# A state-space layer: GpSimd's tensor work moved to VectorE, ScalarE and TensorE, and shorter PSUM tenancies

One NeuronCore of a Trainium2 chip. The metric is the device time of one execution in microseconds (us), lowest is best; "the kernel before" and "the new kernel" are the two sides of the change. The kernel keeps its working tiles in SBUF, the large on-chip memory, and TensorE's products go to PSUM, of which it uses 8 banks; the tenancy of a PSUM tile is the time for which it keeps its banks. The granted clock is the share of full speed that the throttle granted TensorE.

## The reference, cut to what matters

The program is a convolution and attention block, then a bidirectional Mamba layer, then a recurrent layer, on 4 images of 128 channels and 64x64 points. Only the Mamba layer is touched: per direction, 4096 tokens, 4 heads of 64, state of 64.

```python
def _mamba3(x, in_proj, conv_w, conv_b, A_log, dt_bias, D, norm_w, out_proj):
    z, xbc, dt = jnp.split(x @ in_proj, [D_INNER, D_INNER + CONV_DIM], axis=-1)
    xp = jnp.pad(xbc, ((0, 0), (K - 1, 0), (0, 0)))
    xbc = silu(sum((xp[:, i:i + l, :] * conv_w[:, i] for i in range(K))) + conv_b)   # 4 taps
    xh, Bm, Cm = jnp.split(xbc, [D_INNER, D_INNER + D_STATE], axis=-1)
    dt = softplus(dt + dt_bias)
    y = _ssd(xh, dt, -exp(A_log), Bm, Cm) + xh * D      # scores with decays, state carried over chunks
    yg = y * silu(z)
    yn = yg * rsqrt(mean(yg * yg, -1) + EPS) * norm_w
    return yn @ out_proj
```

The kernel uses chunks of 128 tokens, both directions in one pass: 32 chunks an image, 128 in all. Below, "the gate" is the product with silu(z), "the root" the inverse square root of the mean square, BT the transposed B, xdt the inputs times dt, xdd the same times the decay to the chunk's end, and "the exponents" the differences of cumulated decays that the exponential is taken of. Projections and taps are made for groups of four chunks.

## The kernel before: the parts that matter

```python
psj = tile_pool(name="m_psj", bufs=2, space=PSUM)   # projections, one bank each
pst = tile_pool(name="m_pst", bufs=1, space=PSUM)   # tr: 1 bank, pS: 1 bank
psy = tile_pool(name="m_psy", bufs=2, space=PSUM)   # py: 2 banks, twice

def convolved(r, g, i, xc):
    pp = bank()                                     # projection of 512 tokens (cut)
    act(raw[:, i, PAD:], pp, AF.Copy)               # after the pad: gpsimd memset or copy of 3 columns
    nc.gpsimd.tensor_scalar(xc[:, i, :], raw[:, i, PAD:], cw[:, i, PAD:KC], cb[:, i], ALU.mult, ALU.add)
    for tap in range(PAD):
        nc.vector.scalar_tensor_tensor(
            xc[:, i, :], raw[:, i, tap : tap + MG], cw[:, i, tap : tap + 1], xc[:, i, :], ALU.mult, ALU.add)

def front(r, c):                                    # chunk c: all that does not need the state
    # 4 DMA of the cumulated decays into cbc; 4 transposes into ptr; xdt = ptr * dt on VectorE
    nc.gpsimd.tensor_tensor(xdd, xdt, tail, ALU.mult)
    nc.tensor.transpose(py[:, 0, DI + P :], xc[:, 0, cols], k.ident); act(BT, py[:, 0, DI + P :], AF.Copy)
    for d in range(ND): nc.tensor.matmul(py[:, d, DI : DI + P], ...)         # scores, then gm = scores * tri
    for d in range(ND):
        for h in range(NHEAD):
            nc.vector.tensor_scalar(lt[:, d, h, :], cbc[:, d, h, :], s1, s1, ALU.min, ALU.subtract)
    act(lt, lt, AF.Exp); nc.vector.tensor_tensor(lt, lt, gm, ALU.mult); act(E, cbc[:, ND], AF.Exp)
    nc.gpsimd.tensor_copy(dec, E[:, :, P - 1 : P]); nc.gpsimd.tensor_tensor(E, E, C, ALU.mult)

def scan(r, c, v, S):                               # 16 products into py, 2 into pS
    nc.gpsimd.tensor_tensor(S1, S, dec, ALU.mult); nc.vector.tensor_tensor(S1, S1, pS, ALU.add)
    # y = xc * D + py (4 on VectorE)
    nc.gpsimd.tensor_tensor(y, y, zs, ALU.mult)     # the gate

def back(b, c, v):
    act(sq, y, AF.Square)
    nc.gpsimd.tensor_tensor(sq[:, :, 0, :], sq[:, :, 0, :], sq[:, :, 1, :], ALU.add)
    # mean square: 2 products into py; rms; root on GpSimd; 4 output products into py; 2 updates of t on VectorE

for c in range(-1, NT + 1):                         # order of issue
    back(b, c - 1, ...); vs[c + 1] = front(r, c + 1); S = scan(r, c, vs[c], S)
    next(pj, None)                                  # a pair of projections with taps, or gate projections
```

## Time and profile before

| | kernel before |
|---|---|
| time, median of 4 runs beside the new kernel | 5501.5 us (5500.4 to 5503.6) |
| the layer, from 3130 us to the last gate less 5 us | 2119 us |
| TensorE in it: busy, idle, granted clock | 1575, 544, 0.69 |
| VectorE, ScalarE, GpSimd busy | 1459, 632, 1099 us |

The layer is cut at the last product with the gate, less 5 us, in every kernel, so that the layers can be compared. Busy is the union of an engine's instructions; idle is the rest of the window. Six of the 128 gate products lie before 3130 us, so the window holds some 122 chunks; where the layer is divided by 128 for a time per chunk, that time is some 5% low.

### The profile page before, as it was taken

The numbers are of one execution on the slowest core, as the hardware profiler recorded it, in microseconds if no ns is written. First come the engines' busy times: TensorE is split into PE (matmuls) and PEld (weight loads), VectorE is DVE, ScalarE is ACT, GpSimd is POOL, SyncE is SP. The second block draws the span as 40 slices with busy tenths as digits, with TensorE's granted clock in tenths as the row PEclk, the third lists the DMA queues.
The fourth block names the chain that finished last, engine by engine and source line by source line (L and its number), as shares of the span: only waits on it lengthen the run. The fifth ranks groups of instructions, "written<-read, shape, count | busy, mean of one in ns | idle before, by whom it ended". The sixth has DMA issues, their size and how long they took to land. (4 is left out here: it accounts for less than half of the span.)

```text
span 5493.2 us, 46592 instructions
## 1 busy us (share of the span) xinstructions
PE 4679.7 (85%) x17552; PEld 2096.2 (38%) x17552; DVE 2544.0 (46%) x4768; ACT 1367.5 (25%) x1959; POOL 1255.0 (23%) x1383
## 2 busy tenths in 40 slices
PE   6999999999999999999997677777777777777777
PEld 2333333333333333333333334443344334434446
DVE  4222232223232323232323866676657676777665
ACT  2112121212121211121211322332233322322245
POOL 0000000000000000000000555455545554555530
PEclk9999999999999999999997776667766776777678
DMA  2000000000000000000000211111112121121101
GB/s 103 0 0 0 0 1 0 0 0 0 0 0 0 0 0 0 0 0 0 0 0 11 54 43 47 43 47 46 47 40 49 46 47 41 49 52 47 49 5 63
DMA packets 70716, 128.35 MB, mean 23 GB/s; under 512 B 16720, under 2 KB 19664, under 8 KB 69200
## 3 DMA queue, kind: packets, MB, share of 16 engines
q1 hardware_dynamic: 65664, 115.63, 8.0%
q10 hardware_dynamic: 4816, 9.65, 0.5%
q8 instruction: 139, 2.28, 0.2%
q14 instruction: 97, 0.79, 0.1%
HBM read 115.80 MB, written 9.44 MB: 23 GB/s over the span
## 5 line engine op out<-in xcount | busy, mean ns | idle before, releaser
L247 PE MATMUL pc<-xp,w 128*128 128x512 f32 x3136 | 1362.7, 595 | 0.0
L247 PEld LDWEIGHTS pc<-xp,w 128*128 128x128 f32 x3136 | 591.3, 189 | 766.1 <-issue 766.1
L234 DVE TENSOR_TENSOR den<-den,ex 128x1024 f32<-128x1024 f32 x448 | 549.0, 1225 | 665.3 <-ACT ex L225 640.9
L223 PE MATMUL pf<-theta,phi 64*128 64x512 f32 x2048 | 805.8, 629 | 0.0
L225 ACT ACTIVATE ex<-pf 128x1024 f32<-128x1024 f32 x512 | 497.6, 1022 | 793.9 <-PE pf L223 793.9
L254 POOL TENSOR_TENSOR t<-t,r 128x512 f32<-128x512 f32 x32 | 40.4, 1264 | 2690.1 <-ACT r L253 2690.1
L227 PE MATMUL acc<-ex,gT 128*64 128x512 f32 x2048 | 550.6, 617 | 67.5 <-ACT ex L225 67.5
L234 DVE TENSOR_TENSOR den<-ex 128x1024 f32<-128x1024 f32 x32 | 39.2, 1225 | 1169.3 <-ACT ex L225 1169.3
L604 DVE SCALAR_TENSOR_TENSOR xc<-raw,cw,xc 128x512 f32<-128x512 f32 x576 | 476.0, 879 | 204.6 <-POOL xc L602 204.6
L223 PEld LDWEIGHTS pf<-theta,phi 64*128 64x128 f32 x2048 | 250.3, 185 | 546.3 <-issue 545.2
L668 DVE TENSOR_SCALAR lt<-cbc,s 128x128 f32<-128x128 f32 x1024 | 435.2, 477 | 7.7 <-PE py L696 7.6
L253 ACT ACTIVATE r<-pc,bsum 128x512 f32<-128x512 f32 x32 | 22.0, 687 | 1465.6 <-PE pc L251 1465.6
L485 ACT ACTIVATE BT<-py 128x128 f32<-128x128 f32 x128 | 35.5, 277 | 1183.9 <-PE py L654 1183.9
L696 PE MATMUL py<-lt,xdt 128*64 128x128 f32 x2048 | 264.0, 396 | 58.7 <-DVE lt L673 58.2
L736 PE MATMUL py<-wout,y 128*128 128x128 f32 x1024 | 236.3, 371 | 68.5 <-DVE t L739 53.9
L227 PEld LDWEIGHTS acc<-ex,gT 128*64 128x64 f32 x2048 | 102.0, 135 | 468.7 <-ACT ex L225 276.2
L594 PE MATMUL pj<-un,full 128*128 128x512 f32 x256 | 221.7, 972 | 53.9 <-ACT raw L485 47.7
L736 PEld LDWEIGHTS py<-wout,y 128*128 128x128 f32 x1024 | 195.4, 261 | 166.6 <-DVE t L739 84.0
L729 PE MATMUL py<-ones,sq 128*128 128x1 f32 x512 | 105.9, 311 | 179.3 <-POOL sq L726 178.0
L696 PEld LDWEIGHTS py<-lt,xdt 128*64 128x64 f32 x2048 | 169.6, 196 | 201.9 <-DVE lt L673 110.1
L717 POOL TENSOR_TENSOR y<-y,zs 128x512 f32<-128x512 f32 x128 | 164.3, 1283 | 305.7 <-DVE y L714 299.0
L602 POOL TENSOR_SCALAR xc<-raw,cw,cb 128x512 f32<-128x512 f32 x192 | 220.7, 1158 | 42.5 <-ACT raw L485 42.4
(190 smaller groups left out, 5076.7 us busy)
## 6 DMA issues: line engine op xcount, KB each, us to landing
cbc<-csd SPq DMA_DIRECT2D x256, 256.0 KB, 4.5
cbc<-csd SPq DMA_DIRECT2D x256, 128.0 KB, 4.5
t<-in_x SPq DMA_DIRECT2D x4, 2048.0 KB, 26.5
out<-t SPq DMA_DIRECT2D x2, 2048.0 KB, 18.3
out<-t ACTq DMA_DIRECT2D x2, 2048.0 KB, 18.5
w<-in_w7t ACTq DMA_DIRECT2D x1, 3136.0 KB, 15.5
w<-in_w5t ACTq DMA_DIRECT2D x1, 1600.0 KB, 23.8
csd<-cs SPq DMA_DIRECT2D x16, 64.0 KB, 1.6
```

The costliest lines, as they stand in the source:

```text
L223: nc.tensor.matmul(pf[:, h, :], phi[half, m, :], theta[half, cols], start=True, stop=True)
L225: nc.scalar.activation(ex, pf, AF.Exp, scale=scale)
L227: nc.tensor.matmul(acc[h * IC : (h + 1) * IC], gT[:, 2 * m + h, :], ex[:, h, :], start=(m == 0), stop=(m == NT // 2 - 1),)
L234: nc.vector.tensor_tensor(den, ex0 if m == 1 else den, ex, ALU.add)
L247: nc.tensor.matmul(pc, w7[:, y, x, :], xp[:, q * RW + y : (q + 1) * RW + y, x : x + W], start=(y + x == 0), stop=False,)
L594: nc.tensor.matmul(pp, full[:, d, DI + h * P : DI + (h + 1) * P], own(r["un"], d, g), start=True, stop=True)
L602: nc.gpsimd.tensor_scalar(xc[:, i, :], raw[:, i, PAD:], cw[:, i, PAD:KC], cb[:, i], ALU.mult, ALU.add)
L604: nc.vector.scalar_tensor_tensor(xc[:, i, :], raw[:, i, tap : tap + MG], cw[:, i, tap : tap + 1], xc[:, i, :], ALU.mult, ALU.add)
L668: nc.vector.tensor_scalar(lt[:, d, h, :], cbc[:, d, h, :], r["s1"][:, d, c, h : h + 1], r["s1"][:, d, c, h : h + 1], ALU.min, ALU.subtract,)
L696: nc.tensor.matmul(o, v["xdt"][:, d, h, :], v["lt"][:, d, h, :], start=True, stop=S is None)
L717: nc.gpsimd.tensor_tensor(y, y, zs[:, :, :, cols], ALU.mult)
L736: nc.tensor.matmul(po, y[:, d, h, :], wout[:, d, h, :], start=(h == 0), stop=(h == 1))
```

## The change

Its intent is to empty GpSimd's queue of all but the gate, the roots and a few small fixes, and to let the next chunk's front begin without the last one's back. The core of the diff:

```diff
-            act(raw[:, i, PAD:], pp, AF.Copy)
-            nc.gpsimd.tensor_scalar(xc[:, i, :], raw[:, i, PAD:], cw[:, i, PAD:KC], cb[:, i], ALU.mult, ALU.add)
+            act(xc[:, i, :], pp, AF.Identity, scale=cw[:, i, PAD:KC], bias=cb[:, i])
             for tap in range(PAD):
+                o = PAD - tap
                 nc.vector.scalar_tensor_tensor(
-                    xc[:, i, :], raw[:, i, tap : tap + MG], cw[:, i, tap : tap + 1], xc[:, i, :], ALU.mult, ALU.add
+                    xc[:, i, o:], pp[:, 0 : MG - o], cw[:, i, tap : tap + 1], xc[:, i, o:], ALU.mult, ALU.add
                 )
+            nc.vector.tensor_copy(ends[g % 2][:, i, :], pp[:, MG - PAD :])
+            # (once a group: six small GpSimd operations add the last group's ends to the first 3 columns)
...
-            py = v["py"] = psy.tile([P, ND, NC], F32, tag="py", name="py")      # held from scores to output
+            pf = pst.tile([P, ND, NC], F32, tag="pf", name="pf")                # transposes and scores; py in scan, po in back
-            nc.gpsimd.tensor_tensor(xdd, xdt, r["tail"]..., ALU.mult)
+            nc.vector.tensor_tensor(xdd, px, r["tail"]..., ALU.mult)            # tail is multiplied by dt beforehand
...
-                    nc.vector.tensor_scalar(lt[:, d, h, :], cbc[:, d, h, :], s1, s1, ALU.min, ALU.subtract)
-            act(lt, lt, AF.Exp)
+                    if d == 0:
+                        nc.vector.tensor_scalar(x, x, s1, 0.0, ALU.add, ALU.max)
+                    else:
+                        act(x, x, AF.Relu, bias=s1)
+            act(cbc, cbc, AF.Exp, scale=-1.0)
-            nc.gpsimd.tensor_tensor(E, E, xc[:, 1, cols]..., ALU.mult)
+            nc.vector.tensor_tensor(CE, E, xc[:, 1, cols]..., ALU.mult)
...
-                nc.gpsimd.tensor_tensor(S1, S, v["dec"]..., ALU.mult)
-                nc.vector.tensor_tensor(S1, S1, pS, ALU.add)
+                for h in range(NHEAD):
+                    nc.vector.scalar_tensor_tensor(S1[:, h, :], S[:, h, :], v["E"][:, h, P - 1 : P], pS[:, h, :], ALU.mult, ALU.add)
...
-            nc.gpsimd.tensor_tensor(sq[:, :, 0, :], sq[:, :, 0, :], sq[:, :, 1, :], ALU.add)
+            # mean square: 4 accumulating products in place of 2 (8 records of the trace a chunk in place of 4)
...
-                if c >= 1: back(...)        # was ahead of front and scan
                 front(...); scan(...)
+                if c >= 1: back(...)        # now behind them
```

Not shown: the decays are stored negated; exponents and decays are worked in place in cbc, which gets three buffers in place of two; and GpSimd's copy of the last decay (dec, 85 us) falls away.

More of the change, by code (lines that the diff above doesn't have):

```diff
@@ L470, in mamba @@
             nc.vector.tensor_tensor(wout, wout, nw.unsqueeze(3).to_broadcast([P, ND, 2, P]), ALU.mult)
-        raw = wp.tile([P, 6, PAD + MG], F32, name="raw")
+        ends = [wp.tile([P, 6, PAD], F32, name=f"ends{i}") for i in range(2)]
         unp = ctx.enter_context(tc.tile_pool(name="m_un", bufs=NG + 2))
@@ L480, in mamba @@
         pst = ctx.enter_context(tc.tile_pool(name="m_pst", bufs=1, space=PSUM))
-        psy = ctx.enter_context(tc.tile_pool(name="m_psy", bufs=2, space=PSUM))
         def act(out, in_, func, **kw):
@@ L562, in prepare @@
             act(tail, pa, AF.Exp)
+            nc.vector.tensor_tensor(tail, tail, dt, ALU.mult)
             pc = bank()[:, 0 : ND * NT * NHEAD].rearrange(dims, d=ND, c=NT)
@@ L572, in prepare @@
                 cs = tmp.tile([P, 2 * P], F32, tag="cs", name="cs", bufs=2)
-                nc.vector.tensor_copy(cs, pr)
+                nc.vector.tensor_scalar(cs, pr, -1.0, None, ALU.mult)
                 for i in range(2):
@@ L596, in convolved @@
                 )
-            if g == 0:
-                nc.gpsimd.memset(raw[:, i, 0:PAD], 0.0)
-            else:
-                nc.gpsimd.tensor_copy(raw[:, i, 0:PAD], raw[:, i, MG : MG + PAD])
-            act(raw[:, i, PAD:], pp, AF.Copy)
-            nc.gpsimd.tensor_scalar(xc[:, i, :], raw[:, i, PAD:], cw[:, i, PAD:KC], cb[:, i], ALU.mult, ALU.add)
+            act(xc[:, i, :], pp, AF.Identity, scale=cw[:, i, PAD:KC], bias=cb[:, i])
             for tap in range(PAD):
+                o = PAD - tap
                 nc.vector.scalar_tensor_tensor(
-                    xc[:, i, :], raw[:, i, tap : tap + MG], cw[:, i, tap : tap + 1], xc[:, i, :], ALU.mult, ALU.add
+                    xc[:, i, o:], pp[:, 0 : MG - o], cw[:, i, tap : tap + 1], xc[:, i, o:], ALU.mult, ALU.add
                 )
+            nc.vector.tensor_copy(ends[g % 2][:, i, :], pp[:, MG - PAD :])
         def project(r, g):
@@ L615, in project @@
                 convolved(r, g, i + 1, xc)
-                yield
+                if i < 4:
+                    yield
+            if g > 0:
+                for tap in range(PAD):
+                    n = PAD - tap
+                    m = grp.tile([P, 6, PAD], F32, tag="m", name="m")
+                    nc.gpsimd.tensor_tensor(
+                        m[:, :, 0:n], ends[(g - 1) % 2][:, :, tap:], cw[:, :, tap : tap + 1].to_broadcast([P, 6, n]), ALU.mult
+                    )
+                    nc.gpsimd.tensor_tensor(xc[:, :, 0:n], xc[:, :, 0:n], m[:, :, 0:n], ALU.add)
+            yield
             for i in range(0, 6, 2):
@@ L634, in front @@
             xc, _ = r[g]
-            v = {}
-            cbc = wk.tile([P, ND + 1, NHEAD, P], F32, tag="cbc", name="cbc")
+            cbc = wk.tile([P, ND + 1, NHEAD, P], F32, tag="cbc", name="cbc", bufs=3)
             for d in range(ND):
@@ L640, in front @@
                 nc.sync.dma_start(cbc[d * DS : (d + 1) * DS, ND], src[1:2].to_broadcast([DS, NHEAD, P]))
-            ptr = pst.tile([P, ND, DI], F32, tag="tr", name="ptr")
+            pf = pst.tile([P, ND, NC], F32, tag="pf", name="pf")
             for i in range(4):
-                nc.tensor.transpose(ptr[:, i // 2, bass.ts(i % 2, P)], xc[:, 2 + i, cols], k.ident)
-            heads = [P, ND, NHEAD, HD]
-            xdt = wk.tile(heads, F32, tag="xdt", name="xdt")
-            nc.vector.tensor_tensor(
-                xdt, ptr.rearrange("p d (h c) -> p d h c", h=NHEAD),
-                r["dt"][:, :, c, :].unsqueeze(3).to_broadcast(heads), ALU.mult,
-            )
@@ L650, in front @@
-            xdd = wk.tile(heads, F32, tag="xdd", name="xdd")
-            nc.gpsimd.tensor_tensor(xdd, xdt, r["tail"][:, :, c, :].unsqueeze(3).to_broadcast(heads), ALU.mult)
-            py = v["py"] = psy.tile([P, ND, NC], F32, tag="py", name="py")
-            nc.tensor.transpose(py[:, 0, DI + P :], xc[:, 0, cols], k.ident)
-            BT = wk.tile([P, P], F32, tag="BT", name="BT")
-            act(BT, py[:, 0, DI + P :], AF.Copy)
+                nc.tensor.transpose(pf[:, i // 2, bass.ts(i % 2, P)], xc[:, 2 + i, cols], k.ident)
@@ L657, in front @@
+            nc.tensor.transpose(pf[:, 0, DI + P :], xc[:, 0, cols], k.ident)
             for d in range(ND):
                 half = slice(d * DS, (d + 1) * DS)
-                nc.tensor.matmul(py[:, d, DI : DI + P], xc[half, 0, cols], xc[half, 1, cols], start=True, stop=True)
+                nc.tensor.matmul(pf[:, d, DI : DI + P], xc[half, 0, cols], xc[half, 1, cols], start=True, stop=True)
+            heads = [P, ND, NHEAD, HD]
+            px = pf[:, :, 0:DI].rearrange("p d (h c) -> p d h c", h=NHEAD)
@@ L660, in front @@
+            xdt = wk.tile(heads, F32, tag="xdt", name="xdt")
+            nc.vector.tensor_tensor(xdt, px, r["dt"][:, :, c, :].unsqueeze(3).to_broadcast(heads), ALU.mult)
+            xdd = wk.tile(heads, F32, tag="xdd", name="xdd")
+            nc.vector.tensor_tensor(xdd, px, r["tail"][:, :, c, :].unsqueeze(3).to_broadcast(heads), ALU.mult)
             gm = wk.tile([P, ND, P], F32, tag="gm", name="gm")
             nc.vector.tensor_tensor(
-                gm, py[:, :, DI : DI + P], k.tri.unsqueeze(1).to_broadcast([P, ND, P]), ALU.mult
+                gm, pf[:, :, DI : DI + P], k.tri.unsqueeze(1).to_broadcast([P, ND, P]), ALU.mult
@@ L663, in front @@
             )
-            lt = wk.tile([P, ND, NHEAD, P], F32, tag="lt", name="lt")
             for d in range(ND):
                 for h in range(NHEAD):
-                    nc.vector.tensor_scalar(
-                        lt[:, d, h, :], cbc[:, d, h, :],
-                        r["s1"][:, d, c, h : h + 1], r["s1"][:, d, c, h : h + 1], ALU.min, ALU.subtract,
-                    )
-            act(lt, lt, AF.Exp)
-            nc.vector.tensor_tensor(lt, lt, gm.unsqueeze(2).to_broadcast([P, ND, NHEAD, P]), ALU.mult)
@@ L674, in front @@
-            E = wk.tile([P, NHEAD, P], F32, tag="E", name="E")
-            act(E, cbc[:, ND], AF.Exp)
-            dec = wk.tile([P, NHEAD, 1], F32, tag="dec", name="dec")
-            nc.gpsimd.tensor_copy(dec, E[:, :, P - 1 : P])
-            nc.gpsimd.tensor_tensor(E, E, xc[:, 1, cols].unsqueeze(1).to_broadcast([P, NHEAD, P]), ALU.mult)
-            v.update(xdt=xdt, xdd=xdd, BT=BT, lt=lt, dec=dec, CE=E)
-            return v
+                    x, s1 = cbc[:, d, h, :], r["s1"][:, d, c, h : h + 1]
@@ new lines, in front @@
+                    if d == 0:
[3 more added lines that the diff above has]
+            act(cbc, cbc, AF.Exp, scale=-1.0)
+            BT = wk.tile([P, P], F32, tag="BT", name="BT")
+            act(BT, pf[:, 0, DI + P :], AF.Copy)
+            lt, E = cbc[:, 0:ND], cbc[:, ND]
+            nc.vector.tensor_tensor(lt, lt, gm.unsqueeze(2).to_broadcast([P, ND, NHEAD, P]), ALU.mult)
@@ L682, in scan @@
+            CE = wk.tile([P, NHEAD, P], F32, tag="CE", name="CE")
+            nc.vector.tensor_tensor(CE, E, xc[:, 1, cols].unsqueeze(1).to_broadcast([P, NHEAD, P]), ALU.mult)
+            return dict(xdt=xdt, xdd=xdd, BT=BT, lt=lt, E=E, CE=CE)
         def scan(r, c, v, S):
@@ L686, in scan @@
             xc, zs = r[g]
-            py = v["py"]
+            py = pst.tile([P, ND, NC], F32, tag="py", name="py")
             pS = pst.tile([P, NHEAD, HD], F32, tag="pS", name="pS")
@@ L707, in scan @@
             else:
-                nc.gpsimd.tensor_tensor(S1, S, v["dec"].to_broadcast([P, NHEAD, HD]), ALU.mult)
-                nc.vector.tensor_tensor(S1, S1, pS, ALU.add)
+                for h in range(NHEAD):
+                    nc.vector.scalar_tensor_tensor(
+                        S1[:, h, :], S[:, h, :], v["E"][:, h, P - 1 : P], pS[:, h, :], ALU.mult, ALU.add
+                    )
             y = wk.tile([P, ND, 2, P], F32, tag="y", name="y")
@@ L721, in back @@
         def back(b, c, v):
-            y, py = v["y"], v["py"]
+            y = v["y"]
+            po = pst.tile([P, NC], F32, tag="po", name="po")
             sq = wk.tile([P, ND, 2, P], F32, tag="sq", name="sq", bufs=1)
             act(sq, y, AF.Square)
-            nc.gpsimd.tensor_tensor(sq[:, :, 0, :], sq[:, :, 0, :], sq[:, :, 1, :], ALU.add)
-            pms = py[:, 0, DI : DI + ND]
+            pms = po[:, ND * P : ND * P + ND]
             for d in range(ND):
-                nc.tensor.matmul(pms[:, d : d + 1], sq[:, d, 0, :], k.ones[:, 0:1], start=True, stop=True)
+                for h in range(2):
+                    nc.tensor.matmul(
+                        pms[:, d : d + 1], sq[:, d, h, :], k.ones[:, 0:1], start=(h == 0), stop=(h == 1)
+                    )
             rms = wk.tile([P, ND], F32, tag="rms", name="rms")
@@ L733, in back @@
             for d in range(ND):
-                po = py[:, d, DI + P : DI + 2 * P]
+                pd = po[:, bass.ts(d, P)]
                 for h in range(2):
-                    nc.tensor.matmul(po, y[:, d, h, :], wout[:, d, h, :], start=(h == 0), stop=(h == 1))
+                    nc.tensor.matmul(pd, y[:, d, h, :], wout[:, d, h, :], start=(h == 0), stop=(h == 1))
                 i = c if d == 0 else NT - 1 - c
                 tt = t[:, ds(b * T + i * P, P)]
-                nc.vector.scalar_tensor_tensor(tt, po, rms[:, d : d + 1], tt, ALU.mult, ALU.add)
+                nc.vector.scalar_tensor_tensor(tt, pd, rms[:, d : d + 1], tt, ALU.mult, ALU.add)
         def run(gen):
@@ L770, in mamba @@
                         pj = project(r1, 0)
-                if c >= 1:
-                    back(b, c - 1, vs.pop(c - 1))
                 if f < NT:
@@ L776, in mamba @@
                     S = scan(r, c, vs[c], S)
+                if c >= 1:
+                    back(b, c - 1, vs.pop(c - 1))
                 next(pj, None)
```

## The prediction

> **What bounds the kernel now.** The busy digits of the page come first, to find the stage that the change touches (40 slices of 137 us each; only `mamba`, the state-space layer, is changed).
>
> ```profile
> PE   6999999999999999999997677777777777777777
> DVE  4222232223232323232323866676657676777665
> POOL 0000000000000000000000555455545554555530
> PEclk9999999999999999999997776667766776777678
> ```
>
> From the 23rd slice VectorE jumps from 2 to 6 or 7 tenths, GpSimd from 0 to 5, and the granted TensorE clock falls. That is the layer: about 3130 to 5260 us, some 2130 us or 39% of the span. It runs 128 chunks (4 images of 32), so 16.6 us each. The window totals, next, have columns window, length, then busy us (and instructions) of PE, PE weight loads, DVE, ACT, POOL, then granted clock, DMA share and GB/s:
>
> ```profile
> 0.00:3130.00 3130.00, 2926.10 (x8552) 1079.54 (x8554) 938.13 (x1023) 613.71 (x709) 120.89 (x144) 0.98 0.02 7
> 3130.00:5260.00 2130.00, 1581.02 (x8042) 892.82 (x8038) 1462.90 (x3170) 633.00 (x993) 1102.06 (x1206) 0.69 0.18 45
> ```
>
> In the layer's row (the second) no engine is full: TensorE 74% at a clock of 0.69, VectorE 69%, GpSimd 52%, ScalarE 30%. Over 128 chunks that is 12.4, 11.4, 8.6 and 4.9 us of work in 16.6. So the stage is bound by engines that wait for one another, in order. Who waits is in the waits of 3200 to 5200 us (2000 us; columns: waiter, who is waited for, us, times, longest):
>
> ```profile
> DVE t L739 <- PE py L736: 182.3, 147, 3.0
> DVE xc L604 <- POOL xc L602: 182.3, 160, 5.7
> DVE rms L731 <- PE py L729: 52.5, 32, 3.8
> DVE gm L661 <- PE py L659: 42.9, 44, 1.8
> ...
> PE py L729 <- POOL sq L726: 151.4, 78, 3.7
> ...
> PE py L654 <- DVE t L739: 41.6, 94, 0.7
> PE py L659 <- ACT BT L485: 38.5, 109, 0.4
> ```
>
> VectorE loses 182 us to the convolution's first tap, which GpSimd makes, and some 280 us to the output chain of the chunk before (square sum on GpSimd, mean square, output product, update of t). TensorE's L654 waits for t because one PSUM tile, py, holds a chunk from its score product to its output product, and has two copies: the front of chunk c+1 can't start before the back of c-1 is done. The chain of work that ended last shows the same ring, in one pass of it:
>
> ```profile
> 4953.91 1.33 POOL E L678
> 4955.24 3.08 POOL xc L602 x2
> 4958.32 0.58 POOL S L708
> 4958.90 1.14 POOL sq L726
> 4960.04 0.04 issue
> 4960.08 1.01 PE py L729 x4
> ```
>
> GpSimd holds six microseconds of it without a break: it is busy half the time but everything queues behind it.
>
> **What the Trainium skill says.** (1) "SBUF — State Buffer", Who interferes with whom: a VectorE instruction with two SBUF inputs, or in its two-port mode, contends with GpSimd's reads. The trace agrees: adding two 128x1024 tensors takes 1225 ns in the first stage (L234), where GpSimd idles, and 1465 ns here (L673); a tap seen alone takes 750 ns and 879 on average. (2) "ScalarE: Activation LUTs", What ACT_TABLE_LOAD costs: each per-partition operand adds about 93 ns. The trace agrees: a 128x128 activation with a bias takes 368 ns (L900), without 277 (BT). (3) "PSUM — Partial Sum Buffer" says GpSimd cannot reach PSUM, and to guard PSUM by bank. This is why the old kernel copies the projection to SBUF first; the banks are counted below. (4) "TensorE: Matmul & The Clock Gate", Part 1: the clock gate follows how busy TensorE has been. Here it is 0.98 in the dense first stage and 0.69 in this one, so a denser TensorE may also get faster.
>
> **The change part by part**, in busy us over the stage, from these rows of the page and the grouped instructions:
>
> ```profile
> L604 DVE SCALAR_TENSOR_TENSOR xc<-raw,cw,xc 128x512 f32<-128x512 f32 x576 | 476.0, 879 | 204.6 <-POOL xc L602 204.6
> L668 DVE TENSOR_SCALAR lt<-cbc,s 128x128 f32<-128x128 f32 x1024 | 435.2, 477 | 7.7 <-PE py L696 7.6
> L729 PE MATMUL py<-ones,sq 128*128 128x1 f32 x512 | 105.9, 311 | 179.3 <-POOL sq L726 178.0
> L602 POOL TENSOR_SCALAR xc<-raw,cw,cb 128x512 f32<-128x512 f32 x192 | 220.7, 1158 | 42.5 <-ACT raw L485 42.4
> ```
>
> GpSimd loses L602 221, E times C 187 (128 x 1.46), xdd 135, square sum 117, decayed state 85, dec 85 and the pad copies 78: 908 us. It gets the fix of the first three columns: 28 groups x 6 small operations x an estimated 0.6 us (the small dec and raw copies take 0.45 to 0.67), 100 us. It ends near 330 of 1130.
>
> VectorE: the taps read PSUM and one SBUF tensor. The same operation from PSUM on 128 columns takes 351 ns (L739); a column costs 1.01 ns (xdt: 680 ns for 512 columns of PSUM, gm: 422 for 256), so 384 more make 351 + 387, about 740. I use 745. So 576 x (879-745) saves 77. Half of the 1024 exponents leave: 218. The other 512 run against a quieter GpSimd, 342 instead of 477 ns (342 is what a like operation of that shape, L833, takes in the last stage): 69, of which I count 50, since neighbours overlap (the group's 435 us are 425 each, not 477). L673 back to 1230 ns saves 30. Added: xdd 128 x 0.68 (as xdt, same form) = 87; CE 128 x 0.69 = 88; the state in four operations of 64 columns, 4 x 0.284 (351 less 64 columns) against one of 0.41 = 93; the saved ends 192 x 0.15 = 29. Sum -375 + 297 = -78: from 1463 busy to about 1385, 10.8 us a chunk. The intent is not less VectorE work, but less waiting.
>
> ScalarE: the projection's Copy gets two per-partition operands, 192 x 0.18 = +35; 512 Relus at 0.37 = +189; one exponential of 1536 columns instead of two (1.05 and 0.62) saves the fixed part of one, an estimated 0.19, so 24. +200, from 4.9 to 6.5 us a chunk: under half busy.
>
> TensorE: the square sum moves into the mean-square product, 512 more records like L729: +106 us, all of it on an engine that is at 75%. Nothing else is added. 12.4 becomes 13.2 us a chunk at the old clock.
>
> PSUM keeps 8 banks: 2 projection, 1 transposes, 1 state, 2 x 2 py become 2 projection, 2 pf, 2 py, 1 state, 1 po. The front no longer waits for the back of two chunks ago, and the back now comes after the scan, with a whole chunk of slack for gate, square and root. The price: a projection bank is held through the first tap (0.77), three taps (2.2) and the saved ends (0.15), 3.2 us where it was 0.6.
>
> The scheduled order of the new kernel shows what runs beside what in a chunk with projection. First half: VectorE does xdt, xdd, gm, four exponents, S, y, lt and CE (0.68 + 0.68 + 0.42 + 1.37 + 1.14 + 1.36 + 1.23 + 0.69 = 7.6 us, near 7 with overlap). TensorE does the projection pair (4 records, 0.5 each where the timeline shows the clock full and 1.0 where not: 2 to 4), five transposes (1), the mean square (8 x 0.15 = 1.2), scores (0.5 to 0.8) and state products (1.1): 5.8 to 8.1. Second half: VectorE does the root's input, six taps, two updates of t and two ends (0.15 + 4.5 + 0.7 + 0.3 = 5.6); TensorE the scan and output products (timeline: 16 x 0.141 + 16 x 0.089 + 8 x 0.153 = 4.9). The halves are close, so each engine waits a little in turn. Every fourth chunk has no taps, but the gate's projections.
>
> **The sum.** VectorE's waits come to some 600 us of 2000 now. The 182 for L602 and 23 for the state go, and of the 305 for the back and front products I take half away; new waits for PSUM give some back. That leaves 300 to 450 us idle beside 1385 busy, a stage of 1690 to 1840, or 13.2 to 14.4 us a chunk. TensorE needs 13.2 at the old clock; as it gets denser I put its clock at 0.75 to 0.8 and its work at 12.3 us, a guess from the two stages' clocks. I choose 13.9 us a chunk: 2.7 x 128 = 345 us saved, 5500 - 345 = 5155.
>
> **The rivals.** *PSUM takes the wait over*: both projection banks are held by taps, and transposes of the next image and the gate's projections share them, so TensorE, strictly in order, stops before them. For it: 3.2 us of tenancy, five times the old. Against: the order gives the taps the whole scan as cover. At 1.5 us in each of 96 projecting chunks it costs 145 us: 5300. *ScalarE joins the chain*: its order is Relus, exponential, transposed B, square, first taps, each behind a different engine, so a late DMA or exponent delays the taps. For: +200 us. Against: it is idle 70% now. 1.5 us a chunk would make 5345. *Balance better than I think*: clock near 0.85 and VectorE at 90%: 12.3 us a chunk, 4950. *TensorE bound*: its +106 at an unmoved clock and 95% use gives 13.9, the same time as mine but a different story. Slower than before needs over 3 us of new waits a chunk.
>
> **Range and chances.** Between the two bad rivals together (5400) and the good one (4950), with most weight on single effects: 5030 to 5320. Faster by over 2% means under 5390: 0.89; within 0.09; slower 0.02.
>
> **What would show it.** Right: GpSimd near 15% of the stage, VectorE over 78%, taps near 745 ns, the remaining exponents near 345, L654-like waits for t gone, clock above 0.72. Wrong: long waits of TensorE for VectorE before the projection (first rival), of VectorE's lt or taps for ScalarE (second), taps in PSUM well above 745 ns, or a clock that stays at 0.69 with TensorE over 90% busy (the fourth).

## The result, and the profile after

The new kernel takes 5139.9 us (median of 4 runs, 5129.3 to 5152.5) beside 5501.5. Ratios here are the mean time of one kernel's fast runs over that of the other's fast runs of the same rounds, so not quite the ratio of the medians quoted. It is 0.9343 (95% interval 0.9322 to 0.9364). The prediction was 5155, range 5030 to 5320.

Busy digits of the page of the new kernel, 128 us a slice:

```profile
PE   6999999999999999999999968888888888888877
...
DVE  4231322323123232322323157767676767677765
...
POOL 0000000000000000000000001111111111111120
PEclk9999999999999999999999967878787878788888
```

GpSimd has gone from 5 tenths to 1; TensorE is up from 7 to 8, and its clock from 6 or 7 to 7 or 8. Window totals of the layer (columns as in the prediction), the kernel before, then the new kernel:

```profile
3130.00:5249.00 2119.00, 1574.68 (x8008) 888.37 (x8005) 1458.79 (x3148) 632.37 (x992) 1098.58 (x1202) 0.69 0.18 46
```

```profile
3130.00:4892.00 1762.00, 1472.24 (x8427) 915.23 (x8427) 1262.45 (x3415) 791.57 (x1350) 286.94 (x405) 0.81 0.22 54
```

The layer is 357 us shorter, the kernel about as much, so nothing else moved. Read on TensorE, the difference splits without a remainder: its idle time falls from 544 to 290 us (-254) and its busy time from 1575 to 1472 (-102), although it has 512 records more. The busy time falls with the higher clock: the durations of all its records in the layer sum to 3476 us before and to 3008 after without the added mean-square records, 13.5% less; in inverse proportion to the clocks, 0.695 and 0.806, it would be 13.8%. The projection products show it most strongly, in the groups of the page of the kernel before and of the new one:

```profile
L594 PE MATMUL pj<-un,full 128*128 128x512 f32 x256 | 221.7, 972 | 53.9 <-ACT raw L485 47.7
```

```profile
L594 PE MATMUL pj<-un,full 128*128 128x512 f32 x256 | 141.6, 661 | 52.9 <-DVE ends L603 42.7
```

972 ns each have become 661, for the same 256 records. Not every group follows: the output products take 371 ns before (L736) and 376 after (L742). Now the groups of the new kernel (window 3130 to 4900, shapes kept apart), for the prediction's terms:

```profile
L733 PE MATMUL po<-ones,sq 128*128 128x1 f32 x976 | 154.3, 279 | 1.6 <-DVE t L745 1.6
L484 ACT ACTIVATE cbc<-cbc,s 128x128 f32<-128x128 f32 x484 | 153.4, 394 | 2.4 <-DMA cbc<-csd 2.4
...
L678 DVE TENSOR_TENSOR cbc<-cbc,gm 128x1024 f32<-128x1024 f32 x121 | 150.0, 1240 | 36.9 <-ACT cbc L484 36.9
...
L671 DVE TENSOR_SCALAR cbc<-cbc,s 128x128 f32<-128x128 f32 x484 | 131.2, 330 | 34.0 <-DMA cbc<-csd 34.0
L600 DVE SCALAR_TENSOR_TENSOR xc<-pj,cw,xc 128x511 f32<-128x511 f32 x176 | 129.8, 741 | 0.0
...
L710 DVE SCALAR_TENSOR_TENSOR S<-S,cbc,pS 128x64 f32<-128x64 f32 x476 | 102.7, 274 | 0.0
...
L620 POOL TENSOR_TENSOR m<-ends,cw 128x12 f32<-128x12 f32 x26 | 6.6, 255 | 1.8
```

And the waits of the new kernel, 3200 to 4840 us (1640 us), VectorE's, TensorE's and one of ScalarE's:

```profile
DVE t L745 <- PE po L742: 191.4, 167, 2.7
DVE xdt L659 <- PE pf L655: 67.4, 23, 5.0
...
PE pf L651 <- ACT BT L484: 80.2, 62, 2.9
PE pS L702 <- ACT BT L484: 65.2, 27, 4.4
PE pj L594 <- DVE ends L603: 34.2, 55, 1.6
...
ACT BT L484 <- DVE gm L663: 206.6, 34, 8.1
```

No engine waits for GpSimd's taps, state or square sum any more. VectorE still waits for output products. New is that TensorE waits 145 us for BT, ScalarE's copy of the transposed B. In 65 of them it is the state product (L702), which needs BT. The other 80 are the next chunk's transposes (L651), which need nothing of BT but its place: pf has one copy, and BT is read out of it, after VectorE's gm from the same tile. That is PSUM tenancy again. The chain that ended last shows a second way in which BT comes late, once in a group of four chunks (start, length, what):

```profile
4517.87 1.17 ACT cbc L484 x4
4519.03 9.85 issue
4528.89 1.48 ACT cbc L484
4530.37 0.17 ACT BT L484
4530.54 0.04 issue
4530.59 1.12 PE pS L702 x4
```

After its four Relus ScalarE stands 9.85 us. The view calls it "issue", but the timeline has the answer: VectorE runs its own four exponents of that chunk from 4527.93 to 4528.80, because the scheduler put them behind taps and xdt, and the exponential needs them. BT could have run at 4528.02, when gm was done, but it stands behind that exponential in ScalarE's queue, and TensorE's state product behind BT.

### The profile page after: what moved, and what is told of

It reads as the page before. It is cut to its first block, busy times and chain, and to the rows that moved or that the text cites. A ratio compares the mean times of both kernels' runs of the same rounds, so it can differ in the third digit from the quotient of the medians.

```text
span 5138.3 us, 47952 instructions
## 1 busy us (share of the span) xinstructions
PE 4588.5 (89%) x18064; PEld 2131.6 (41%) x18064; DVE 2342.6 (46%) x5080; ACT 1540.2 (30%) x2343; POOL 390.0 (8%) x531
## 5 line engine op out<-in xcount | busy, mean ns | idle before, releaser
L600 DVE SCALAR_TENSOR_TENSOR xc<-pj,cw,xc 128x510 f32<-128x510 f32 (+2 forms) x576 | 411.6, 739 | 2.8 <-ACT xc L484 2.8
L697 PE MATMUL py<-cbc,xdt 128*64 128x128 f32 x2048 | 325.2, 344 | 15.8 <-DVE y L717 8.0
L484 ACT ACTIVATE cbc<-cbc 128x1536 f32<-128x1536 f32 x128 | 189.9, 1483 | 198.4 <-issue 195.9
L697 PEld LDWEIGHTS py<-cbc,xdt 128*64 128x64 f32 x2048 | 204.4, 168 | 107.1 <-issue 46.9
L742 PE MATMUL po<-wout,y 128*128 128x128 f32 x1024 | 243.1, 376 | 5.2 <-DVE t L745 3.5
L702 PE MATMUL pS<-xdd,BT 128*64 128x256 f32 x512 | 147.7, 504 | 84.8 <-ACT BT L484 75.8
L742 PEld LDWEIGHTS po<-wout,y 128*128 128x128 f32 x1024 | 183.4, 253 | 79.8 <-issue 51.3
L745 DVE SCALAR_TENSOR_TENSOR t<-po,rms,t 128x128 f32<-128x128 f32 x256 | 89.7, 351 | 259.4 <-PE po L742 216.3
L651 PE MATMUL pf<-ident,xc 128*128 128x128 f32 x512 | 106.9, 324 | 101.2 <-ACT BT L484 98.5
L594 PE MATMUL pj<-un,full 128*128 128x512 f32 x256 | 141.6, 661 | 52.9 <-DVE ends L603 42.7
```

Of the source, the lines that this page charges most:

```text
L484: tc.keep_in_program_order(nc.scalar.activation(out, in_, func, **kw))
L594: nc.tensor.matmul(pp, full[:, d, DI + h * P : DI + (h + 1) * P], own(r["un"], d, g), start=True, stop=True)
L600: nc.vector.scalar_tensor_tensor(xc[:, i, o:], pp[:, 0 : MG - o], cw[:, i, tap : tap + 1], xc[:, i, o:], ALU.mult, ALU.add)
L697: nc.tensor.matmul(o, v["xdt"][:, d, h, :], v["lt"][:, d, h, :], start=True, stop=S is None)
L702: nc.tensor.matmul(pS[d * DS : (d + 1) * DS], v["BT"][:, d * DS : (d + 1) * DS], v["xdd"][:, d], start=True, stop=True)
L742: nc.tensor.matmul(pd, y[:, d, h, :], wout[:, d, h, :], start=(h == 0), stop=(h == 1))
```

## The experiments

Eleven of the kernels below are the new kernel with an edit, one is the kernel before with an edit; all gave correct results and were timed in three rounds against the kernel before. "Against new" is the difference of the ratios times 5500 us; the new kernel's own ratio is 0.9343. Each ratio is uncertain by 9 to 12 us either way, and where batches differ, ratios of different chips are compared, so a difference under some 15 us is not shown; the 17 us of u_taps are at that edge. The layer's columns are the window totals as above, of the one profiled run; it is some 20 us off the median for u_sq (5199, slow side) and d_set (5237, fast side), up to 16 for the others.

| run | ratio (95%) | against new | layer us | TensorE busy / idle, clock | VectorE | GpSimd |
|---|---|---|---|---|---|---|
| before | 1 | +361 | 2119 | 1575 / 544, 0.69 | 1459 | 1099 |
| new | 0.9343 (0.9322 to 0.9364) | 0 | 1762 | 1472 / 290, 0.81 | 1262 | 287 |
| u_taps | 0.9374 (0.9358 to 0.9390) | +17 | 1766 | 1461 / 305, 0.80 | 1313 | 555 |
| u_gates | 0.9296 (0.9279 to 0.9313) | -26 | 1723 | 1457 / 266, 0.81 | 1120 | 731 |
| u_exps | 0.9393 (0.9377 to 0.9409) | +28 | 1781 | 1474 / 307, 0.81 | 1364 | 288 |
| u_psum | 0.9358 (0.9343 to 0.9374) | +8 | 1778 | 1458 / 320, 0.78 | 1278 | 302 |
| u_sq | 0.9404 (0.9389 to 0.9420) | +34 | 1823 | 1481 / 342, 0.78 | 1310 | 440 |
| u_taps_gates | 0.9526 (0.9510 to 0.9542) | +101 | 1860 | 1535 / 325, 0.76 | 1283 | 980 |
| u_pool | 0.9831 (0.9815 to 0.9847) | +268 | 2020 | 1531 / 489, 0.72 | 1260 | 1065 |
| b_psum | 0.9787 (0.9771 to 0.9804) | +244 | 2021 | 1574 / 447, 0.71 | 1399 | 1059 |
| d_set | 0.9561 (0.9545 to 0.9577) | +120 | 1859 | 1508 / 351, 0.78 | 1309 | 1062 |
| d_read | 0.9735 (0.9719 to 0.9751) | +216 | 1993 | 1574 / 419, 0.75 | 1469 | 1023 |
| d_pe | 0.9596 (0.9575 to 0.9616) | +139 | 1883 | 1614 / 269, 0.79 | 1263 | 289 |
| n_gates | 0.9248 (0.9232 to 0.9265) | -52 | 1717 | 1464 / 253, 0.82 | 1140 | 728 |

### One part undone at a time

The theory at this point: waits, on GpSimd's queue and on the PSUM tile, were the cost. The rival, which the windows suggest at first sight: VectorE lost some 200 us of work, and the gain is that.

u_taps:

```diff
-            act(xc[:, i, :], pp, AF.Identity, scale=cw[:, i, PAD:KC], bias=cb[:, i])
+            # pad by GpSimd, then:
+            act(raw[:, i, PAD:], pp, AF.Copy)
+            nc.gpsimd.tensor_scalar(xc[:, i, :], raw[:, i, PAD:], cw[:, i, PAD:KC], cb[:, i], ALU.mult, ALU.add)
             # the three taps on VectorE read raw again; no ends, no fix of the first columns
```

> The new kernel with one part undone: the projection is copied to SBUF by ScalarE, the first tap is made by GpSimd, the other taps read SBUF (as before); everything else stays new. It puts about 300 us back on GpSimd and some 64 us on VectorE (taps at 826 ns busy each instead of 715, if the contention comes back). My theory (the time was in waits on GpSimd and on the PSUM tile, not in VectorE's work): VectorE waits for GpSimd's first tap again, 130 to 180 us; time 5270 to 5320. Rival (the gain is the 198 us of VectorE work that fell away): only the 64 us come back, about 5205.

Measured: 5147 us, +17. Both theories expected more. VectorE waits 17 us for GpSimd's first tap (31 times), where it waited 182 before: GpSimd, with only this and the gate to do, is early.

u_gates:

```diff
-            nc.vector.tensor_tensor(tail, tail, dt, ALU.mult)
-            nc.vector.tensor_tensor(xdd, px, r["tail"]..., ALU.mult)
+            nc.gpsimd.tensor_tensor(xdd, xdt, r["tail"]..., ALU.mult)
-            nc.vector.tensor_tensor(CE, E, ..., ALU.mult)
+            nc.gpsimd.tensor_tensor(CE, E, ..., ALU.mult)
-                    (four scalar_tensor_tensor for S1)
+                nc.gpsimd.tensor_tensor(S1, S, v["E"][:, :, P - 1 : P]..., ALU.mult)
+                nc.vector.tensor_tensor(S1, S1, pS, ALU.add)
```

> The new kernel with xdd, E times C and the decayed state put back on GpSimd (the state is then added on VectorE); everything else stays new. GpSimd gets about 400 us, VectorE loses about 220 (xdd 82, E times C 83, three of four state operations 54). My theory: the scan again waits for GpSimd, and the ring through GpSimd comes back in part: slower, 5200 to 5290. Rival (VectorE work sets the time): faster by 100 to 200, 4950 to 5040.

Measured: 5105 us, 26 faster than new. My theory has the sign wrong. The rival has the sign but not the size: VectorE lost 142 us of work and the time 26. So this part of the change, by itself, does harm.

u_exps:

```diff
-                    if d == 0:
-                        nc.vector.tensor_scalar(x, x, s1, 0.0, ALU.add, ALU.max)
-                    else:
-                        act(x, x, AF.Relu, bias=s1)
+                    nc.vector.tensor_scalar(x, x, s1, 0.0, ALU.add, ALU.max)
```

> The new kernel with all eight exponents of a chunk on VectorE, as before, none on ScalarE. VectorE gets 512 x 0.3 = 150 us, ScalarE loses 153. My theory (VectorE is 71% busy, so part of it falls into idle time; ScalarE's late exponential may even wait longer for VectorE): +60 to +100, 5200 to 5240. Rival (VectorE work sets the time): +150 or more, 5290.

Measured: 5159 us, +28, with 101 us more work on VectorE. Less than either expected. With u_gates it rules the rival out: 101 us more VectorE work cost 28, 142 less gained 26.

u_psum:

```diff
+        psy = tile_pool(name="m_psy", bufs=2, space=PSUM)
+            ptr = pst.tile([P, ND, DI], F32, tag="tr", name="ptr")          # x transposes only
-            pf = pst.tile([P, ND, NC], F32, tag="pf", name="pf")
+            pf = psy.tile([P, ND, NC], F32, tag="py", name="py")            # also used by scan and back
+                if c >= 1: back(...)      # ahead of front again
```

> The new kernel with the old tenancy and order: transposes in a bank of their own, one double-buffered two-bank tile that holds a chunk from score product to output product, and the back of chunk c-1 issued ahead of the front of chunk c+1. No engine's work changes. My theory: TensorE's transposed B and scores wait for t again and VectorE for the output chain; half of the old 305 us: 5260 to 5320, and the granted clock falls below 0.78 in the layer. Rival (work on VectorE): no change, 5140.

Measured: 5143 us, +8, and the intervals overlap: no difference shown. The waits do come back (TensorE's transposed B for t 49 us, VectorE's rms for the mean square 91 us), but they replace others. The expected 120 to 180 us were wrong.

So no single part pays, and my theory in its first form falls. Either none of these matters, or they stand in for one another.

### Parts undone together, and the other side

> The new kernel with everything that left GpSimd put back on it together: copy and first tap, xdd, E times C, decayed state, square sum. New stay the PSUM tiles, their order and the exponents' halves. First four runs: each undone part alone cost nothing (0.930 to 0.939 of the kernel before, against 0.934), so the parts stand in for one another. Theory now: GpSimd's in-order queue binds only when it carries all of it (about 1000 us of the layer); then 5330 to 5480. Rival: the PSUM tenancy together with any lighter part is what counts; then GpSimd's load doesn't matter and the time stays 5140 to 5200.

u_pool is u_taps, u_gates and u_sq (next) in one; the dec copies stay out, so not quite everything is back. Measured: 5406 us, +268: three quarters of the whole gain is lost by three edits that cost 17, -26 and 34 alone. GpSimd carries 1065 us (1099 before). TensorE's waits of u_pool, 3200 to 4800 us:

```profile
PE po L722 <- POOL sq L719: 158.7, 76, 5.3
PE pf L642 <- ACT BT L484: 94.5, 44, 5.5
PE pS L693 <- ACT BT L484: 84.0, 21, 5.7
```

The square sum is there a simple addition, but it stands at the end of a full queue and TensorE stands behind it, 151 us in the kernel before too.

u_sq:

```diff
             act(sq, y, AF.Square)
+            nc.gpsimd.tensor_tensor(sq[:, :, 0, :], sq[:, :, 0, :], sq[:, :, 1, :], ALU.add)
-            (mean square from both halves, 4 products)
+            (mean square from sq[:, d, 0, :], 2 products)
```

> The new kernel with the square sum alone back on GpSimd (117 us there; TensorE loses half of the mean-square records, about 77 us). GpSimd theory: not loaded enough to bind, so 5100 to 5150 and, as TensorE is 84% busy, perhaps a gain of up to 40. Rival (this one step was the critical one, since it stands in the output chain): 5200 to 5280.

Measured: 5175 us, +34: between the two expectations. In the profiled run, which is 24 us above the median, TensorE has 457 records fewer and is still busy 9 us longer, at a clock of 0.78, and it waits 62 us for the sum.

b_psum:

```diff
 (the kernel before)
-        psy = tile_pool(name="m_psy", bufs=2, space=PSUM)
+        (front writes transposes and scores to pf, scan has its own py, back its own po, all single; back is issued last)
```

> The kernel before with the new PSUM tiles and the new order alone (front, scan, back; tiles pf, py, po); no engine's work changes. GpSimd theory: the ring through GpSimd stays, 5400 to 5500. PSUM rival: most of the gain comes, 5150 to 5280.

Measured: 5385 us, 117 faster than the kernel before (ratio 0.9787). Lower than the GpSimd theory's 5400, far above the rival's 5280. With GpSimd full, the PSUM part is worth 117 us; with GpSimd empty (u_psum) nothing that shows. That is the mark of two waits of which either can be the last.

u_taps_gates (u_taps and u_gates together, square sum left on TensorE):

> The new kernel with taps and the three gate operations back on GpSimd, but the square sum still on TensorE (two parts that each cost nothing alone). About 960 us on GpSimd. Load theory: nearly as slow as with the square sum too (5406), 5330 to 5400. Chain theory (the square sum behind the full queue makes TensorE wait for the mean square, its longest wait there): 5200 to 5280.

Measured: 5237 us, +101: within the chain theory's range. GpSimd is nearly as full as in u_pool (980 against 1065 us), yet 167 us are still won. The square sum, which costs 34 us in a nearly empty queue, costs 167 in a full one.

### Is it the load of the queue, or what is in it?

```diff
+            nc.gpsimd.tensor_copy(idle[:, 0:1], xf[:, 0:1])         # xf is xdt, flat: ties the load to the chunk
+            for _ in range(12):
+                nc.gpsimd.memset(idle, 0.0)                         # d_set: 128x512, 0.53 us each
+            # d_read instead: for _ in range(5): nc.gpsimd.tensor_tensor(idle, xf, xf, ALU.add)
```

d_set, then d_read:

> As the run with idle additions, but with twelve fills of a tile per chunk in place of the five additions (128x512, an estimated 0.53 us each from 0.21 us for 128 columns and 0.27 for 210): about the same load on GpSimd, nothing read from SBUF, so hardly any contention with VectorE. Load theory: as slow as the additions, 5300 or more. Chain theory: 5135 to 5170. The difference between the two runs is what contention costs.

> The new kernel with idle work for GpSimd: in each chunk, after xdt, one small copy and five additions of xdt to itself (128x512, some 1.3 us each) into a tile that nobody reads; 128 x 6.6 = 850 us, so GpSimd is as full as in the kernel before (about 1150 us of the layer), and its reads contend with VectorE's. Load theory (a full in-order queue on GpSimd is enough, whatever is in it, because gate and root stand behind it): 5300 to 5450. Chain theory (what cost was that the scan, the taps and the mean square waited for results that GpSimd made one after another): gate and root have a chunk of slack, so only contention shows, 5150 to 5220.

Measured: d_set 5255 us (+120), d_read 5355 us (+216). The load theory gave d_read's range but wanted d_set as slow; the chain theory fits neither. Load that nobody waits for costs 120 us. Gate and root stand behind it: VectorE waits 103 us for the root (37 in the new kernel), so a chunk of slack isn't enough for a queue that is over half full. But the fills also slow VectorE, which is busy 47 us longer for the same work, so not all of the 120 is the queue. About the same load as reads costs 96 more, with VectorE busy another 160 us: contention. VectorE's rows for the exponents (L676) and for the product of decay and score (L683), d_set, then d_read (window 3130 to 4900):

```profile
L676 DVE TENSOR_SCALAR cbc<-cbc,s 128x128 f32<-128x128 f32 x464 | 166.1, 478 | 35.1 <-DMA cbc<-csd 35.1
L683 DVE TENSOR_TENSOR cbc<-cbc,gm 128x1024 f32<-128x1024 f32 x114 | 142.6, 1251 | 43.2 <-ACT cbc L485 43.2
```

```profile
L676 DVE TENSOR_SCALAR cbc<-cbc,s 128x128 f32<-128x128 f32 x428 | 184.4, 488 | 29.4 <-DMA cbc<-csd 29.4
L683 DVE TENSOR_TENSOR cbc<-cbc,gm 128x1024 f32<-128x1024 f32 x106 | 182.9, 1726 | 23.7 <-ACT cbc L485 23.6
```

With two inputs in SBUF the product takes 1240 ns in the new kernel, 1251 beside fills and 1726 beside reads. The exponents, with one SBUF input, take 330, 478 and 488: they meet both. These are means of two kinds: the median is 279 to 282 ns in all three runs, and what grows is the share that takes over 500 ns, 7% in the new kernel and 35% and 28% here. So a part of them waits long and most do not wait at all. This fits the rule of which the prediction quotes a part, its two cases side by side: two inputs meet reads only, the two-port mode meets fills too. That the exponents run in that mode no view shows.

### Is TensorE the bound now?

```diff
+            (the four mean-square products again, into columns 300 and 301 of po, read by nobody)
```

> The new kernel with the mean-square products doubled: four more per chunk (eight records like the 0.158 us ones), written to unused columns of the same bank, read by nobody; 154 us of TensorE more. If TensorE (84% busy at a clock of 0.81) bounds the layer now: +100 to +150, 5240 to 5290. If the waits between the engines bound it: +20 to +60.

Measured: 5269 us, +139 for an expected 154 us of TensorE work, which shows as 141 us more busy time in the layer. The work comes through almost in full: TensorE's idle time falls only from 290 to 269 us. So TensorE's queue bounds the new kernel: with 84% busy, the rest is gaps that the added work doesn't fill. One rival is left: the added products stand in the output chain, VectorE's wait for the mean square grows from 32 to 119 us, and the same work at another place of the queue was not tried. Over the table the clock mostly rises as the idle share falls: 26% idle at 0.69 (before), 24% at 0.72 (u_pool), 21% at 0.75 (d_read), 16% at 0.81 (new), 15% at 0.82 (n_gates). It is no strict rule: u_taps_gates has 17% at 0.76 and d_pe 14% at 0.79.

### A faster version

n_gates is u_gates with the order mended that the chain after showed: exponents first in the front, BT ahead of the exponentials on ScalarE.

```diff
 (u_gates, and in front)
+            (the eight exponents here, ahead of the transposes)
             pf = pst.tile([P, ND, NC], F32, tag="pf", name="pf")
 ...
+            act(BT, pf[:, 0, DI + P :], AF.Copy)
             act(cbc, cbc, AF.Exp, scale=-1.0)
-            act(BT, pf[:, 0, DI + P :], AF.Copy)
```

> A try for a faster kernel: the new one with xdd, E times C and the decayed state on GpSimd (which ran at 0.930), and in the front the exponents first and transposed B ahead of the exponentials on ScalarE, so that the exponential and TensorE's state product wait less for VectorE (8 to 10 us once in four chunks in the profile, with 65 us of TensorE behind it). If those waits count: 5030 to 5080. If TensorE's own work binds: unchanged at 5105.

Measured: 5091 us, ratio 0.9248, 1.0% below the new kernel and 0.5% below u_gates (intervals apart, though of another batch). TensorE waits only 9 us for BT (120 in u_gates) and idles 253 us in place of 266; it waits 58 us for the square instead, which now comes after BT and then the exponential. The result is short of the 5030 to 5080 hoped for: one wait on an in-order queue was exchanged for a smaller one.

## Why the prediction was right or wrong, point by point

**The time** is right: 5155 predicted, 5140 measured; 13.9 us a chunk against 13.8 (both low by the same 5%).

**What bounded it before** is right in kind. GpSimd's queue held everything up, though only half busy: give it back its taps, gate operations and square sum and 268 of 361 us are lost. What I did not foresee is that the parts replace each other. I priced L602's 182 us of waits as a sum to be taken off; undone alone, that part costs 17 us. With 731 us in the queue nothing is lost (u_gates), with 980 it is 101 (u_taps_gates), with 1065 and the square sum in it 268. What is in the queue counts as well as how much: TensorE stands behind the square sum. One reading was off: of the 280 us given to the output chain, the lines shown hold 235; the other 43 are gm's wait for the scores, a product of the front.

**"Of the 305 for the back and front products I take half away"** fails. Per chunk they come to 2.5 us before (305 of 2000 us) and 2.4 after (191 + 67 + 32 of 1640). PSUM tenancy was real in the kernel before (b_psum: 117 us) and is nothing that shows in the new one (u_psum).

**VectorE's sum** was mis-sized: -78 predicted, -196 measured in the layer (1459 to 1262). Durations were right: taps 745 predicted and 739 measured, exponents 342 and 330 (in part luck: their median is 279 in the new form, with one per-partition operand, and was 337 in the old, with two), product 1230 and 1240, state 284 and 274. Too small was the gain on the exponents, 268 against 296 (435 less 139), and too large the state's addition, 93 against about 57, since I took mean times although four neighbours overlap. The rows of these terms, scaled to 128 chunks, make -130. All VectorE rows of the two layer windows make -145 (1555 to 1411), and the other 51 us are overlap of neighbours of different rows, which the union counts once: 97 us of it before, 148 after. In its place VectorE's idle time was too small, 300 to 450 predicted and 500 measured, so that it is busy 72% of the layer and not over 78%. The two errors cancel, so the time came out right for a partly wrong reason.

**TensorE** is the bound, which I listed as a rival ("the same time as mine but a different story") and described wrongly: not 95% busy at an unmoved clock, but 84% busy at 0.81. d_pe shows it, up to the rival named there. Its added work was 56 us (162 against 106 for the mean square, scaled to 128 chunks) where I had 106; the clock I guessed at 0.75 to 0.8. My sum ran over VectorE and did not use the clock, though TensorE's busy time fell by 102 us with it.

**GpSimd's rest** is right, 287 us for 330; the small fixes take 0.21 to 0.26 us, not 0.6. **ScalarE's** addition is 159 us for 200; the Relus took 162 of the 189 allowed.

**The rivals.** The projection banks hold TensorE up little: 53 us of waits for the ends before projections and gates, 145 feared. But the 80 us at L651 are PSUM tenancy too, at a tile that the rival did not name. ScalarE in the chain is half right: a late BT costs TensorE 145 us of waits, and moving it gained half a per cent. The upper end of the range was mis-added: the two bad rivals together make 5155 + 145 + 190 = 5490, not 5400.

**What stays open.** How u_pool's 268 us split between load, contention and dependence: the idle-load runs give 120 and 96 for loads of that size, but not of that mix. And the last 93 us between u_pool and the kernel before belong to PSUM, the exponents, the dec copies, cbc's third buffer and their combination; for PSUM b_psum gives 117 us, the others were not tried on the kernel before. What sets TensorE's clock beyond its idle share is open too.

## What to carry to other kernels

An engine that is half busy can be the bound if its in-order queue holds one link of several engines' chains; undoing single parts of a cure then shows little, and only undoing them together shows the cause. Read the gain on the engine that ends up as the bound, idle and busy time apart: here the denser TensorE also ran at a higher clock, and 102 of 357 us came as less busy time. Once that engine is the bound, work moved elsewhere to unload a third one (here the gate operations, to VectorE) can be moved back at a profit.

## What the Trainium skill lacked or had wrong

- "TensorE: Matmul & The Clock Gate", Part 1, puts the ramp penalty at under 1% of a typical span, said of the warm-up at a kernel's start. It gives no figure for a stage that loses its clock again and again through short waits. Here the layer's mean clock went from 0.69 to 0.81 with fewer waits on other engines, and TensorE's busy time fell 102 us of 5500 (1.9%) with 512 records more. Before, the trace's clock records stand at half for 1292 of 2119 us (683 of 1762 after), though no gap of TensorE there is longer than 4.6 us.
- "GPSIMD Engine Reference" times an addition of 2048 columns and a loop of 512 elements, but no tile of a few columns, no power and no fill. Measured: 0.21 to 0.26 us for products and sums of 128x6 to 128x18, 0.71 us for a power of 128x2, 0.53 us for a fill of 128x512.
- "ScalarE: Activation LUTs", Rules for kernel authors, sends relu and additions to VectorE; its comparison is for bf16. For the 128x128 fp32 exponents here the gap is small, in busy time: 153.4 us for 484 on ScalarE, 0.32 each, and 131.2 for 484 on VectorE, 0.27 each.
